# The Newton step of the reciprocal root in three VectorE instructions instead of four

## The chip, the cores and the metric

The kernel runs on one core of a Trainium2 chip. A core has a matrix engine (PE, whose weight loads are shown apart as PEld), a vector engine (DVE), an activation engine (ACT) and a general engine (POOL), all with instruction queues of their own that are worked off in order; SP's queue issues nearly all transfers (DMA). Intermediate values lie in SBUF (128 partitions) and in PSUM, where PE writes. The metric is the device time of one execution in microseconds (us); lower is better. The time stated is the median of several executions.

## The reference

The input `x` has 4 sequences of 256 tokens with 256 features, so 1024 tokens. Two decoder layers add to it, each with attention, a state-space block (mamba) that reads a second input `ctx_1024`, and a feed-forward part, each after a layer norm. All is float32. The change touches two places where a reciprocal square root is needed. The first is layer 0's attention, whose heads of 32 features are normalised (8 query, 2 key and 2 value heads):

```python
def _layernorm_unit(x, eps=EPS):
    mu = jnp.mean(x, axis=-1, keepdims=True)
    xc = x - mu
    var = jnp.mean(xc * xc, axis=-1, keepdims=True)
    return xc * jax.lax.rsqrt(var + eps)
...
q = _layernorm_unit(q) * SCALAR
k = _layernorm_unit(k)
v = _layernorm_unit(v)
```

The second is layer 1's mixture of 32 experts, of which 6 act on each token:

```python
def step(acc, ew):
    w1, w2, g = ew
    h = jnp.square(jax.nn.relu(xf @ w1.T)) @ w2.T
    return (acc + g[:, None] * h, None)
```

The kernel multiplies the hidden units by the square root of the gate `g` before they are squared, so it needs `sqrt(g)`, which it makes as `g * rsqrt(g)`.

## The kernel before, in words

Tokens lie in 8 tiles of 128 on the partitions; a batch (one sequence) is two tiles. The source calls the instructions in an order that serves as their priority. A scheduler then sets the order of each engine's queue when the kernel is built, by its own estimates of durations and by when operands and buffers come free; at run time each queue is fixed. So a change in some instructions can move others on every queue.

*Layer 0, first stage* (about 25 to 190 us of the profile). For each of the 4 batches `head0(b)` normalises the batch (`ln_transposed`), makes queries, keys and values on PE (L393), rotates them on DVE (L403, L409, L410), takes the mean away (L417, L418), sums the squares (L425, L426) and calls `rsqrt_steps` on the 24 variances of each token pair (2 tiles x 12 heads: a tile of 128x24). The results scale the queries (L433, `qn`) and values (L436, `vn`) on DVE and the keys (L440, `krep`, two instructions per batch) on POOL. `tail0(b)` transposes qn and krep on PE (L461, L466), copies them out on ACT (L471, `qkT`), and makes the scores (L486, L490), tanh (L499) and exp (L507) on ACT, the weighted sums (L513, L523, L524) on PE, the division on DVE (L449 `rden`, L450 `at`), the output projection (L543) and the addition to `x` (L551).

Into this are woven the scans of layer 0's mamba block, 16 states x 2 halves x 2 pairs of batches. A state is: decay on ACT (L238), input product `db` on POOL (L240), the scan on DVE (L241), its product `hc` on DVE (L243); the states are summed by turns on PE (L258) and on POOL (L260 here, L250 in layer 1). Their rows `bt` and `ct` are spread by DMA (L232). `mamba_front` prepares a pair of batches (convolution L189, L202, L203, dt L211 and L213, `du` L216).

*Layer 0's feed-forward* runs in two halves of two batches. For each batch the gate `sz` (ACT, L275) is multiplied on (L286), transposed back and added (L288, L294); then the norm follows: statistics on DVE (L121, L122), four small POOL instructions (L125 to L128), the normalised batch on ACT (L137), transposes on PE (L141), a copy on ACT (L144). Then come the matmuls L643 and L669. The weights of this part take the place of the attention's, so SP's loads L618 (`downs`), L620 (`gw`), L622 (`uw`) and L624 (`dw`) wait for the last projection L543; `dw` is multiplied by `downs` on POOL (L625).

*Layer 1* has attention with 16 heads of 128 features (L714 projections, L734 to L748 rotation, L812 to L845 scores and softmax, L868/L869 weighted sums, L883 output), its scans woven in, and then the experts in two halves (`moe(0)` and `moe(1)`, 512 tokens each). `moe` computes gates (`route`), clamps them (L985), calls `rsqrt_steps` on a tile of 128x128 (4 tiles of tokens x 32 experts), multiplies by the gate (L987), transposes the result on PE (L990), copies it (L992) and writes it to DRAM (L993), from where a row per expert is spread over the partitions (L1006, `gr`). The experts' matmuls are L1015 and L1029, with L1020 on DVE and L1021 on ACT between them.

`rsqrt_steps(v, n)` begins with a start value from the bits of `v` (L105) and makes three Newton steps of four DVE instructions each (L109 to L112) on two small tiles, `rs_r` and `rs_t`. It is called six times: four times with 24 columns, twice with 128.

Of the kernel before, what the change touches and what calls it, by code (L numbers as in the profile page):

```python
# [14 lines left out]
ALU = mybir.AluOpType  # L15
# [26 lines left out]
def decoder_kernel(  # L42
# [27 lines left out]
    nc = tc.nc  # L70
# [30 lines left out]
    def rsqrt_steps(v, n):  # L101

        r_ = small.tile([P, n], F32, tag=f"rs_r{n}", name="rs_r")
        t_ = small.tile([P, n], F32, tag=f"rs_t{n}", name="rs_t")
        nc.vector.tensor_scalar(  # L105
            r_.bitcast(I32), v.bitcast(I32), -0.5, float(0x5F3759DF), ALU.mult, ALU.add
        )
        for _ in range(3):
            nc.vector.tensor_mul(t_, r_, r_)  # L109
            nc.vector.tensor_mul(t_, t_, v)  # L110
            nc.vector.tensor_scalar(t_, t_, -0.5, 1.5, ALU.mult, ALU.add)
            nc.vector.tensor_mul(r_, r_, t_)  # L112
        return r_


# [234 lines left out]
    with ExitStack() as ph:  # L350
# [33 lines left out]
        def head0(b):  # L384
# [40 lines left out]
            nc.vector.tensor_reduce(rs24, sq, AX.X, ALU.add)  # L425
            nc.vector.tensor_scalar(rs24, rs24, 1.0 / 32, 1e-6, ALU.mult, ALU.add)  # L426
            rs = rsqrt_steps(rs24, 24).rearrange("p (c h) -> p c h", c=2)
            qn = ap.tile([P, 2, 8, 32], F32, tag="qn", name="qn")
            krep = ap.tile([P, 2, 2, 4, 32], F32, tag="krep", name="krep")
# [255 lines left out]
    with ExitStack() as ph:  # L685
# [289 lines left out]
        def moe(hf, ps_p, ps_h, acc):  # L975
# [8 lines left out]
            gpos = gp.tile([P, 4 * NE], F32, tag="gpos", name="gpos")  # L984
            nc.vector.tensor_scalar(gpos, gate.rearrange("p t e -> p (t e)"), 1e-30, None, ALU.max)  # L985
            root = rsqrt_steps(gpos, 4 * NE)
            done = nc.vector.tensor_mul(root, root, gate.rearrange("p t e -> p (t e)")).ins  # L987
            pg = ps(ps_p)
# [239 lines left out]
```

## Time and profile before

| what | value |
|---|---|
| median of 3 runs (lowest, highest) | 896.88 us (895.14, 897.36) |
| the profiled execution's own time | 899.26 us |
| its span, first to last instruction | 897.5 us |
| instructions on DVE | 1112 |
| narrow steps, 128x24: L109, L110, L111, L112, 12 each | 399, 304, 477, 284 ns mean |
| wide steps, 128x128: L109, L110, L111, L112, 6 each | 292, 292, 225, 291 ns mean |
| mean granted TensorE clock | 0.941 of full speed |

The profile is one execution. Its page gives the busy time of each engine, the span in 40 equal slices with a digit for the busy tenths of each, the chain of work that ended last, and the costliest groups of instructions. A group's line reads: source line, engine, operation, output <- inputs with partitions x elements and type, count, then busy us and mean ns of one, then idle time of that engine just before these instructions and the work that ended most of it. A line of the timeline reads: start us, duration us, engine, source line, operation, names and shapes, and in brackets the idle time before it with its releaser. "x2" means that two instructions of the same kind that followed each other are shown as one.

Narrow steps appear with durations from 0.16 us to over 1 us, which is why their means differ between lines that do the same amount of work. The profiled execution took 2.38 us more than the median; 1.76 us of its time lie outside the span.

### The profile page before, as it was taken

Reading aid. Unit: us, or ns where it says so; the run is one execution under the profiler, and the core shown is the slowest. Engines: PE = TensorE matmul, PEld = TensorE weight load, DVE = VectorE, ACT = ScalarE, POOL = GpSimd, SP = SyncE. Lnnn points to the kernel's source line nnn. Section 1 sums busy time; section 2 is a strip of 40 time slices with the busy share of each in tenths; the row PEclk is TensorE's granted clock in tenths of the full one; section 3 lists DMA queues with packets and bytes.
Section 4 is the critical chain, followed back from the end, with each engine's and each line's share of the span. In section 5 each row is a group of like instructions: output and inputs, shape, how many; then the busy total and the mean of one; then the engine's idle time right before and its main releaser. Section 6 shows DMA issues by size and latency. Waiting matters only on the chain.

```text
span 897.5 us, 10261 instructions
## 1 busy us (share of the span) xinstructions
PE 803.8 (90%) x3062; PEld 496.9 (55%) x3062; DVE 588.2 (66%) x1112; ACT 480.7 (54%) x1188; POOL 423.2 (47%) x427
## 2 busy tenths in 40 slices
PE   5788989978978989889898978997999999999997
PEld 2345656623433435546565745675666656666665
DVE  4897999775877668777759785788067676212121
ACT  5565545478848736746856693776333433211111
POOL 5654879865779624735635472422257751000000
PEclk9896889778986999999999999998999999999999
DMA  5545465672623400100110010000048743555542
GB/s 165 174 144 212 148 181 195 196 257 76 206 93 102 147 15 24 39 10 30 41 47 24 24 47 1 24 3 21 29 153 225 233 151 101 150 148 159 158 145 82
DMA packets 61015, 98.36 MB, mean 110 GB/s; under 512 B 6352, under 2 KB 26720, under 8 KB 60704
## 3 DMA queue, kind: packets, MB, share of 16 engines
q1 hardware_dynamic: 60080, 96.48, 34.4%
q10 hardware_dynamic: 880, 1.23, 0.4%
q8 instruction: 24, 0.39, 0.2%
q14 instruction: 31, 0.25, 0.1%
HBM read 96.24 MB, written 1.44 MB: 109 GB/s over the span
## 4 chain that ended last, share of the span: by engine, by line
PE 46%; DVE 12%; ACT 5%; POOL 3%; issue 3%; POOLq 0%; DVEq 0%; ACTq 0%
PE ps L1015 13%; PE ps L1029 12%; PE ps L883 5%; PE ps L714 4%; PE ps L868 2%; PE ps L821 2%; DVE ps L741 2%; DVE qs L734 1%; ACT sc L840 1%; DVE qr L742 1%; PE ps L748 1%; DVE h L241 1%; PE ps L669 1%; PE ps L643 1%; POOL sc L845 1%
## 5 line engine op out<-in xcount | busy, mean ns | idle before, releaser
L240 POOL TENSOR_TENSOR db<-bt,du 128x512 f32<-128x512 f32 x128 | 162.7, 1282 | 82.2 <-DVE h L241 57.0
L241 DVE TENSOR_TENSOR_SCAN h<-h,db 128x512 f32<-128x512 f32 x128 | 152.7, 1215 | 29.2 <-ACT h L238 28.1
L1015 PE MATMUL ps<-moe_xnT,w 128*128 128x512 f32 x272 | 128.9, 597 | 0.0
L1029 PE MATMUL ps<-w,hT 128*128 128x256 f32 x544 | 128.5, 379 | 0.0
L1020 DVE SCALAR_TENSOR_TENSOR hT<-ps,gr 128x512 f32<-128x512 f32 x64 | 44.1, 689 | 126.8 <-PE ps L1015 126.8
L238 ACT ACTIVATE h<-dt,negA 128x512 f32<-128x512 f32 x128 | 86.2, 689 | 73.5 <-DVE hc L243 71.2
L1029 PEld LDWEIGHTS ps<-w,hT 128*128 128x128 f32 x544 | 103.0, 190 | 40.2 <-issue 29.4
L1021 ACT ACTIVATE hT<-hT 128x512 f32<-128x512 f32 x68 | 42.8, 629 | 133.8 <-DVE hT L1020 133.6
L714 PE MATMUL ps<-wqkv,xnT 128*128 128x512 f32 x192 | 93.4, 598 | 8.0 <-DVE rq L706 5.6
L243 DVE TENSOR_TENSOR hc<-h,ct 128x512 f32<-128x512 f32 x128 | 84.8, 678 | 3.0 <-DMA ct<-bc 1.8
L250 POOL TENSOR_TENSOR y<-y,hc 128x512 f32<-128x512 f32 x64 | 80.8, 1272 | 8.3 <-DVE hc L243 6.4
L845 POOL TENSOR_TENSOR sc<-sc,rsum 128x512 f32<-128x512 f32 (+1 forms) x32 | 46.2, 1466 | 66.4 <-DVE rsum L843 66.3
L1015 PEld LDWEIGHTS ps<-moe_xnT,w 128*128 128x128 f32 x272 | 51.9, 192 | 36.5 <-issue 33.2
L707 POOL TENSOR_TENSOR rq<-rq,nhalf 128x8 f32<-128x8 f32 x20 | 33.0, 1651 | 80.9 <-DVE rq L706 80.7
L729 ACT ACTIVATE sq<-ps 128x128 f32<-128x128 f32 x160 | 42.4, 282 | 49.4 <-PE ps L714 49.4
L840 ACT ACTIVATE sc<-sc,nm 128x256 f32<-128x256 f32 (+1 forms) x128 | 56.7, 448 | 7.6 <-DVE nm L835 4.2
L883 PE MATMUL ps<-wo,oT 128*128 128x256 f32 x256 | 57.0, 381 | 0.0
L883 PEld LDWEIGHTS ps<-wo,oT 128*128 128x128 f32 x256 | 48.1, 190 | 8.9 <-ACT oT L876 2.6
L714 PEld LDWEIGHTS ps<-wqkv,xnT 128*128 128x128 f32 x192 | 32.7, 190 | 30.1 <-issue 17.5
L258 PE MATMUL ps<-hc,ident 128*128 128x512 f32 x64 | 39.9, 712 | 8.8 <-DVE hc L243 8.8
L260 POOL TENSOR_TENSOR y<-y,hc 128x512 f32<-128x512 f32 x32 | 40.8, 1274 | 4.8 <-DVE rs_t L110 2.1
L748 PE MATMUL ps<-ident,qr 128*128 128x128 f32 x160 | 28.1, 293 | 13.7 <-DVE qr L742 11.8
(206 smaller groups left out, 1450.6 us busy)
## 6 DMA issues: line engine op xcount, KB each, us to landing
bt<-bc SPq DMA_DIRECT2D x96, 256.0 KB, 3.5
ct<-bc SPq DMA_DIRECT2D x96, 256.0 KB, 3.8
w<-in_w_dram SPq DMA_DIRECT2D x64, 256.0 KB, 3.7
gr<-gt SPq DMA_DIRECT2D x64, 256.0 KB, 3.4
wqkv<-in_wqkv_dram SPq DMA_DIRECT2D x1, 3072.0 KB, 11.8
wo<-in_wo_dram SPq DMA_DIRECT2D x1, 2048.0 KB, 9.3
x<-in_x_dram SPq DMA_DIRECT2D x4, 256.0 KB, 5.1
w<-in_ws_dram SPq DMA_DIRECT2D x4, 256.0 KB, 3.9
```

What stands on the lines that cost most here:

```text
L238: nc.scalar.activation(h, dt[:, c, :], AF.Exp, scale=negA[:, a : a + 1])
L240: nc.gpsimd.tensor_mul(db, bt, du[:, c, :])
L241: nc.vector.tensor_tensor_scan(h, h, db, 0.0, ALU.mult, ALU.add)
L243: nc.vector.tensor_mul(hc, h, ct)
L250: nc.gpsimd.tensor_add(y[:, c, :], y[:, c, :], state(n, c, bt, ct))
L714: mm(pq, lhsT=xnT[:, f, c * P : (c + 1) * P], rhs=wqkv1[:, f, ch * 512 : (ch + 1) * 512], start=(f == 0), stop=(f == 1),)
L840: nc.scalar.activation(part, part, AF.Exp, bias=nm[:, qc, j : j + 1], accum_out=rsum[:, qc, j : j + 1])
L845: nc.gpsimd.tensor_mul(part, part, rsum[:, qc, :].unsqueeze(2).to_broadcast([P, 4, w]))
L883: mm(pout[:, c * 256 : (c + 1) * 256], lhsT=oTs[h // 4][:, h % 4, c * P : (c + 1) * P], rhs=wo1[:, 8 * gp + h, :], start=(h == 0), stop=(h ...
L1015: mm(ph_, lhsT=w[:, f * P : (f + 1) * P], rhs=xnT[:, f, :], start=(f == 0), stop=(f == 1))
L1020: gated.append(nc.vector.scalar_tensor_tensor(h, ph_, 0.0, g, ALU.max, ALU.mult).ins)
L1029: mm(po[t // 2][:, (t % 2) * 256 : (t % 2 + 1) * 256], lhsT=h[:, t * P : (t + 1) * P], rhs=w[:, 256:512], start=start and t % 2 == 0, stop ...
```

## The change

Each Newton step is `r <- r * (1.5 - 0.5 * v * r * r)`. Before, DVE squares `r`, multiplies by `v`, forms `-0.5 t + 1.5` and multiplies by `r`. After, the factor -0.5 is taken into the square and the addition of 1.5 into the last product, each with the instruction that applies a scalar and then a second tensor (`scalar_tensor_tensor`):

```diff
         for _ in range(3):
-            nc.vector.tensor_mul(t_, r_, r_)
+            nc.vector.scalar_tensor_tensor(t_, r_, -0.5, r_, ALU.mult, ALU.mult)
             nc.vector.tensor_mul(t_, t_, v)
-            nc.vector.tensor_scalar(t_, t_, -0.5, 1.5, ALU.mult, ALU.add)
-            nc.vector.tensor_mul(r_, r_, t_)
+            nc.vector.scalar_tensor_tensor(r_, t_, 1.5, r_, ALU.add, ALU.mult)
         return r_
```

The start value L105, the three rounds, the tiles and the callers stay. Six calls with three rounds each make 18 instructions less: twelve of 128x24 in layer 0's first stage and six of 128x128 in `moe`.

## Prediction

> **What bounds the kernel now.** I read the page first: the busy times, the 40 slices (22.4 us each) and the chain that ended last.
>
> ```profile
> PE 803.8 (90%) x3062; PEld 496.9 (55%) x3062; DVE 588.2 (66%) x1112; ACT 480.7 (54%) x1188; POOL 423.2 (47%) x427
> ...
> PE   5788989978978989889898978997999999999997
> ...
> DVE  4897999775877668777759785788067676212121
> ...
> PE 46%; DVE 12%; ACT 5%; POOL 3%; issue 3%; POOLq 0%; DVEq 0%; ACTq 0%
> ```
>
> PE is the engine of the whole; the last third is its expert matmuls without a gap. DVE, which the change relieves, counts only where its digits are 9: slices 3 to 8, the first stage, where the four `head0` calls lie. Busy times per stretch (the windows view: us of 30 for PE, PEld, DVE, ACT and POOL, then the granted clock) show that stage more finely:
>
> ```profile
> 90.00:120.00 30.00, 27.05 (x148) 19.87 (x147) 29.82 (x46) 16.50 (x39) 21.77 (x18) 0.84 0.50 159
> 120.00:150.00 30.00, 27.00 (x156) 17.46 (x156) 28.46 (x44) 14.86 (x39) 28.88 (x25) 0.90 0.58 183
> ```
>
> DVE is full in the first; in the second POOL is as full (28.88 of 30). Time taken from DVE before 120 us can become time, but must still get past POOL. Then the groups with different shapes kept apart (busy us, mean ns):
>
> ```profile
> L111 DVE TENSOR_SCALAR rs_t<-rs_t 128x24 f32<-128x24 f32 x12 | 5.7, 477 | 0.1
> ...
> L109 DVE TENSOR_TENSOR rs_t<-rs_r 128x24 f32<-128x24 f32 x12 | 4.8, 399 | 0.1
> ...
> L110 DVE TENSOR_TENSOR rs_t<-rs_t,a_rs 128x24 f32<-128x24 f32 x12 | 3.6, 304 | 0.1
> ...
> L111 DVE TENSOR_SCALAR rs_t<-rs_t 128x128 f32<-128x128 f32 x6 | 1.4, 225 | 0.2
> ...
> L961 DVE SCALAR_TENSOR_TENSOR gate<-em,room 128x128 f32<-128x128 f32 x2 | 0.6, 292 | 0.1
> ```
>
> The means of the narrow steps mislead. The timeline of DVE, and POOL's beside it, show why (start, duration):
>
> ```profile
> 43.58 0.17 DVE L110 TENSOR_TENSOR rs_t<-rs_t,a_rs 128x24 f32<-128x24 f32 x1
> 43.67 0.49 DVE L409 TENSOR_TENSOR ps<-ps,cst 128x320 f32<-128x320 f32 x1
> 44.07 1.03 DVE L111 TENSOR_SCALAR rs_t<-rs_t 128x24 f32<-128x24 f32 x1
> 45.02 1.21 DVE L335 TENSOR_TENSOR diag<-ident,par 128x1024 f32<-128x1024 f32 x1
> ```
> ```profile
> 43.80 1.27 POOL L260 TENSOR_TENSOR y<-y,hc 128x512 f32<-128x512 f32 x1 [1.28 <-DVE rs_t L110]
> ```
>
> A step costs 0.17 us; the L111 at 44.07 took 1.03 because it ended with POOL's L260 (43.80 + 1.27 = 45.07). Removing a step that stood in such a hold hands the hold to the next instruction that has all its operands in SBUF.
>
> **The change part by part.** Twelve 128x24 steps go (4 calls of `head0`, 3 Newton steps each) and six 128x128 (2 calls of `moe`).
>
> *Price of the new form.* The trace has no step with a scalar between two narrow tensors. From below: a 128x24 L110 unheld, 0.17 us; from above: L961, the same form at 128x128, 0.292. L961 costs exactly what the tensor_tensor steps of its size cost (L109, L110 at 128x128: 292 and 292 ns), so I take no extra.
>
> The Trainium skill says otherwise ("Vector Engine (DVE) Microarchitecture Reference", "Points that are easy to get wrong"): this form halves its throughput when both tensors are SBUF and not bf16. By that rule, with 1.22 ns per column from the rows ((292 - 165) / 104), the twelve wide new steps cost 0.156 us more each and the twenty-four narrow ones 0.03: about 0.9 us on `moe` 0's path and 0.7 us in the first stage, and the sum below would read 896.0. L961 speaks against the rule, and I go by L961.
>
> *First stage, the steps themselves.* From start to the next start the twelve narrow L111 take 0.17, 0.95, 0.44, 0.91, 0.08, 0.95, 0.21, 0.21, 0.09, 0.07, 0.62 and 0.24 us: 4.94 in all. Seven are unheld (1.07 us, gone for good); five are held (3.87), and of those only some 0.09 each is the step's own. Surely gone: 1.07 + 5 x 0.09 = 1.5 us.
>
> *First stage, the order.* The scheduler sets each queue's order when the kernel is built, so the shorter chains move other work. In the changed kernel as built, batch 0's qn and vn (L433, L436) stand one scan earlier on DVE, ahead of L417, L418 and a L243; POOL's two krep (L440) and PE's transposes (L461, L466) of that batch move up likewise. This aims at two idle times of before. PE waited 3.23 us (72.38 to 75.61) for L450, which stood behind L433, L436 and a L418 that took 1.36 us beside krep; and DVE, with nothing left to do, waited for PE:
>
> ```profile
> 83.56 0.17 DVE L112 TENSOR_TENSOR rs_r<-rs_r,rs_t 128x24 f32<-128x24 f32 x1
> 87.85 0.21 DVE L449 RECIPROCAL rden<-ps 128x8 f32<-128x8 f32 x1 [4.12 <-PE ps L524]
> ```
>
> I let the 4.12 us go: L449's matmuls come some 4 us earlier if batch 0's tail does. The lead at the stage's end is then 1.5 + 4.1 = 5.6 us. Bounds: 1.5 (only the unheld steps) and 4.94 + 4.12 = 9.1. What is late next there is POOL's L240/L260 stream.
>
> *Start of the first FFN half, the give-back.* Where attention releases its pool (last L543, ends 184.58 + 1.03 = 185.61), SP issues downs, gw, uw and dw. POOL scales dw (L625), and here the order turns against the change: before, the norm of batch 0 (L125 to L128) came first; after, as built, L625 stands ahead of it.
>
> ```profile
> 194.86 0.22 POOL L125 TENSOR_SCALAR ln_nb<-ln_mv 128x2 f32<-128x2 f32 x1 [3.32 <-DVE ln_mv L122]
> ...
> 197.89 3.59 POOL L625 TENSOR_TENSOR dw<-dw,downs 128x1536 f32<-128x1536 f32 x1 [0.24 <-DMA dw<-in_down_dram]
> ```
>
> So POOL blocks on dw's landing, and the norm, L137 on ACT and the transposes L141 behind it queue up. dw is ready 197.89 - 185.61 = 12.28 us after the last L543; then 3.59 for L625, 1.60 for the norm (194.86 to L137's 196.46), 0.65 from L137 to L141 (208.12 to 208.77, the second time). L141 would start at 185.61 + 12.28 + 3.59 + 1.60 + 0.65 = 203.73, against 200.67 before, where it stood behind L211: +3.1 us. From L141 to the first FFN matmul it is 11.0 us, unchanged, with the same order on every engine. All of it moves with the last L543, so the lead comes off: 3.1 - 5.6 = -2.5 us at the FFN's start. ACT also gets two more table loads there (1.28 us each, two others go away near 75 us): they delay L203 and the dt matmuls, at most to 200.67 + 2.56 - 5.6 = 197.6, earlier than L141's 203.73 - 5.6 = 198.1; hidden by the dw wait, and 2.56 us on the path if that wait is gone.
>
> *From there to the end* the orders are equal up to the roots in `moe`, and the stretch is tied through PE; I carry the -2.5 through.
>
> *`moe` 0.* The chain of waits runs through its root (604.07 to 607.46). Before, the last L112 and L987 had been put behind sixteen attention instructions; after, they stand in the chain, ahead of L814. From the first L109 to L814: 607.61 - 604.33 = 3.28 us before; after, nine steps and L987 at 0.325 each (start to start in this chain): 3.25. No gain. The transposes L990 wait in PE's order until 621.77 either way. Price 0; if PE came sooner it would be at most 0.8 (three L111 at 0.26).
>
> *`moe` 1.* 758 to 763 us, under an unbroken row of matmuls (749 to 897): 0, and if that cover were gone, 0.8.
>
> **Sum.** -2.5 us. The profiled execution took 899.26 us (span 897.5), 2.4 above the median; it would take 896.8, and the median 896.88 becomes 894.4. What a measurement here tells from no change is 0.3%, 2.7 us.
>
> **The rivals.**
>
> *A, the sum:* 894.4; by the bounds of the lead (9.1 and 1.5) 890.9 to 898.5.
>
> *B, slower: POOL swallows the lead and dw keeps its price.* Place: 120 to 190 us, where POOL is 96% busy for 30 us and the trace has DVE's holds ending with POOL's instructions. If POOL sets the pace, the last L543 stays, the lead is 0, and the norm still waits for dw: +3.1, 900.0. It is slower by the bound once the lead is under 0.4 us. For it: the window row, and two krep (0.94 us each) now ahead of scan products. Against: POOL was busy only 21.77 of 30 in the window before, so it has room to start early.
>
> *C, the dw wait does not bite:* its load lands earlier, with less traffic in front, or the scheduler's place for it hurts nobody. The lead stays whole, less what the table loads then cost at most: 5.6 to 3.0 off, 891.3 to 893.9; I take 891.3.
>
> *D, nothing arrives:* lead and give-back cancel, or PE, busy 24 to 27 of every 30 us at a clock of 0.75 to 0.90, sets the stage anyway and the norm has slack: 897.
>
> **How the numbers follow.** A 0.40, B 0.29, C 0.17, D 0.14. A straddles the bound of 0.3% (faster is under 894.2): 0.22 faster, 0.15 same, 0.03 slower, as orders that a build moves also lose. C is faster, D the same but for 0.01, B slower. Together faster 0.40, same 0.28, slower 0.32. The 8 in 10: from 890.5, just under the largest lead, to 901.5, B with half of the table loads (1.3 us) on top. A's own range is 890.9 to 898.5.
>
> **What the profile after would show.** DVE with 1094 instructions. The new narrow steps at 0.17 us unheld, the wide ones at 0.29 (0.45 would prove the skill's rule). The 3.23 us of PE at 72 us and DVE's 4.12 at 84 us gone or shrunk; the last L543 near 180 instead of 185.6. L625 before the norm of batch 0, with POOL idle until dw lands; L137 12.28 + 3.59 + 1.6 us after the last L543; first FFN matmul near 209. L987 right behind the last step of the root, L990 still far later. I am wrong if the last L543 does not come earlier (B), if L137 does not wait behind L625 (C), or if the distance from the first FFN matmul to the end changes by more than 1 us, which none of my steps provides for.

## The result and the profile after

The changed kernel takes 903.09 us (median of 5 runs, 900.37 to 904.33) against 896.88 us before (5 runs, 891.43 to 897.36): a ratio of 1.0071, 95% interval 1.0044 to 1.0098. It is slower by 6.2 us. The forecast was 894.4 us, and the range ended at 901.5.

The page of the profile after (an execution of 900.98 us, span 899.2): busy times, then the slices of PE and DVE, then the chain that ended last.

```profile
PE 793.7 (88%) x3062; PEld 491.6 (55%) x3062; DVE 589.0 (66%) x1094; ACT 480.5 (53%) x1188; POOL 421.5 (47%) x427
...
PE   5689789958977989789898978997899999999997
...
DVE  4997899875878668768759785787157776212121
...
PE 46%; DVE 12%; ACT 5%; POOL 3%; issue 3%; DVEq 0%; ACTq 0%; POOLq 0%
```

DVE has lost 18 instructions (1112 to 1094), but not busy time: 588.2 us before, 589.0 after. The groups with shapes kept apart say why (busy us, mean ns; in the changed kernel L109 and L111 are the new form, L110 the product with `v`, and later lines stand one lower than before):

```profile
L109 DVE SCALAR_TENSOR_TENSOR rs_t<-rs_r 128x24 f32<-128x24 f32 x12 | 5.5, 461 | 0.0
L435 DVE TENSOR_TENSOR vn<-r,rs_r 128x128 f32<-128x128 f32 x4 | 4.3, 1086 | 0.0
L110 DVE TENSOR_TENSOR rs_t<-rs_t,a_rs 128x24 f32<-128x24 f32 x12 | 4.1, 344 | 0.0
...
L607 DVE TENSOR_SCALAR wmean<-wmean 128x10 f32<-128x10 f32 x4 | 3.7, 928 | 0.0
L111 DVE SCALAR_TENSOR_TENSOR rs_r<-rs_t,rs_r 128x24 f32<-128x24 f32 x12 | 2.7, 222 | 0.0
L110 DVE TENSOR_TENSOR rs_t<-rs_t,gpos 128x128 f32<-128x128 f32 x6 | 1.8, 292 | 0.2
L111 DVE SCALAR_TENSOR_TENSOR rs_r<-rs_t,rs_r 128x128 f32<-128x128 f32 x6 | 1.8, 292 | 0.2
L109 DVE SCALAR_TENSOR_TENSOR rs_t<-rs_r 128x128 f32<-128x128 f32 x6 | 1.7, 290 | 0.2
```

The wide new form costs 290 to 292 ns, like the plain product. But the values `vn` went from 697 to 1086 ns each, and the small `wmean` scaling from 420 to 928; before they read:

```profile
L436 DVE TENSOR_TENSOR vn<-r,rs_r 128x128 f32<-128x128 f32 x4 | 2.8, 697 | 0.0
L608 DVE TENSOR_SCALAR wmean<-wmean 128x10 f32<-128x10 f32 x4 | 1.7, 420 | 0.0
```

The holds beside POOL have moved to other instructions. To measure them I took, for each DVE instruction of the first stage (24 us to the last L551), what it took beyond the fastest of its own form, where that was over 0.08 us: 13.5 us in all before, 14.4 after.

The milestones of both profiles, in us from the start: where the additions L551 and the first FFN matmul L643 start, where the last L543 ends, the distance from there to L643, and where the last addition to `x`, L1051, starts (lines as before the change):

| | L551 of batches 0, 1, 2, 3 | last L543 ends | first L643 | distance | last L1051 |
|---|---|---|---|---|---|
| before | 95.3, 132.5, 157.5, 185.6 | 185.6 | 211.7 | 26.1 | 892.9 |
| after | 88.2, 133.8, 160.9, 182.7 | 182.7 | 213.7 | 31.0 | 894.6 |

Batch 0 is done 7 us earlier, as hoped. By batch 1 the lead is gone, and behind the last L543 another 5 us are lost. From L643 to the last L1051 it is 681.2 us before and 680.9 after, so in these two profiles everything happens before 214 us. (In the profiles below with the same order from there on, this part took 679 to 684 us; it varies a little from one execution to the next.) The two profiled executions differ by only 1.7 us where the medians differ by 6.2; how that comes is told with the first experiment.

Where the lead goes, DVE's timeline of the changed kernel shows:

```profile
91.04 1.17 DVE L607 TENSOR_SCALAR wmean<-wmean 128x10 f32<-128x10 f32 x1
92.11 1.47 DVE L606 TENSOR_REDUCE wmean<-wqkv 128x10 f32<-128x1280 f32 x1
93.51 2.33 DVE L240 TENSOR_TENSOR_SCAN h<-h,db 128x512 f32<-128x512 f32 x2
95.75 1.26 DVE L242 TENSOR_TENSOR hc<-h,ct 128x512 f32<-128x512 f32 x2
...
103.94 0.49 DVE L402 TENSOR_TENSOR rr<-ps,cst 128x320 f32<-128x320 f32 x1 [3.41 <-PE ps L392]
```

And PE's:

```profile
96.47 1.51 PE L257 MATMUL ps<-hc,ident 128*128 128x512 f32 x2 [2.17 <-DVE hc L242]
...
101.00 2.91 PE L392 MATMUL ps<-wqkv,xnT 128*128 128x384 f32 x4
```

The same four matmuls in the kernel before:

```profile
96.11 1.45 PE L393 MATMUL ps<-wqkv,xnT 128*128 128x384 f32 x4
```

In the changed kernel PE waits 2.17 us for `hc`, which stands behind weight means and scans; a little later its granted clock is 0.50 (98 to 104 us; 1.00 before), the four L392 take 2.91 us where they took 1.45 before, and now DVE waits 3.41 us for PE. The idle times of before (PE 3.23 us at 72 us, DVE 4.12 at 84) did go or shrink (the latter to 2.97 us at 80); these came in their place.

Behind the last L543, POOL first, then DVE, ACT and PE of the changed kernel:

```profile
193.05 3.42 POOL L624 TENSOR_TENSOR dw<-dw,downs 128x1536 f32<-128x1536 f32 x1 [1.66 <-PE ps L210]
196.93 0.22 POOL L124 TENSOR_SCALAR ln_nb<-ln_mv 128x2 f32<-128x2 f32 x1 [0.46 <-DVE ln_mv L121]
```
```profile
193.71 3.04 DVE L285 TENSOR_TENSOR yg<-y,sz 128x256 f32<-128x256 f32 x1
196.67 0.17 DVE L121 BATCH_NORM_AGGREGATE ln_mv<-ln_st 128x2 f32<-128x6 f32 x1
196.76 1.19 DVE L240 TENSOR_TENSOR_SCAN h<-h,db 128x512 f32<-128x512 f32 x1
```
```profile
198.53 1.09 ACT L136 ACTIVATE xn<-x,ln_nb,ln_rs 128x256 f32<-128x256 f32 x2 [4.09 <-POOL ln_nb L127]
```
```profile
198.73 2.07 PE L257 MATMUL ps<-hc,ident 128*128 128x512 f32 x2 [5.72 <-DVE hc L242]
200.74 2.07 PE L210 MATMUL ps<-xdbl,dtproj 8*128 8x512 f32 x2
202.74 1.11 PE L140 MATMUL ps<-ident,xn 128*128 128x128 f32 x4
```

The same `yg` in the kernel before:

```profile
194.28 0.39 DVE L286 TENSOR_TENSOR yg<-y,sz 128x256 f32<-128x256 f32 x1
```

While POOL scales `dw`, DVE's `yg` is held for 3.04 us (0.39 before). Behind it wait the statistics, the scan, `hc`, PE's L257 and, in PE's order, the transposes L140 that lead to the FFN. POOL was idle 1.66 us before L624. The line names PE as the releaser, but SP issued `dw` at 184.31 and it landed 8.6 us later, at 192.9, so POOL did wait for the load. That wait is short; what holds DVE is the scaling.

### The profile page after: what moved, and what is told of

Its sections match the earlier page's. It is cut to its first block, busy times and chain, and to the rows that moved or that the text cites. A ratio compares the mean times of both kernels' runs of the same rounds, so it can differ in the third digit from the quotient of the medians.

```text
span 899.2 us, 10229 instructions
## 1 busy us (share of the span) xinstructions
PE 793.7 (88%) x3062; PEld 491.6 (55%) x3062; DVE 589.0 (66%) x1094; ACT 480.5 (53%) x1188; POOL 421.5 (47%) x427
## 4 chain that ended last, share of the span: by engine, by line
PE 46%; DVE 12%; ACT 5%; POOL 3%; issue 3%; DVEq 0%; ACTq 0%; POOLq 0%
PE ps L1014 12%; PE ps L1028 12%; PE ps L882 5%; PE ps L713 4%; PE ps L867 2%; PE ps L820 2%; DVE ps L740 2%; ACT sc L839 1%; DVE qs L733 1%; DVE qr L741 1%; PE ps L747 1%; DVE h L240 1%; PE ps L668 1%; PE ps L642 1%; POOL sc L844 1%
## 5 line engine op out<-in xcount | busy, mean ns | idle before, releaser
L257 PE MATMUL ps<-hc,ident 128*128 128x512 f32 x64 | 38.8, 693 | 15.3 <-DVE hc L242 15.2
L747 PE MATMUL ps<-ident,qr 128*128 128x128 f32 x160 | 28.1, 294 | 14.6 <-DVE qr L741 12.7
```

## The experiments

The chain of reasons under test: the shorter step saves time; the new order of the first stage and of `dw` costs more. The rivals: the new form itself, or the wide roots in `moe`.

Comparisons are with the kernel before, whose median over the runs beside each group was 897.1, 897.0 and 896.2 us.

**The narrow calls alone.**

```diff
         for _ in range(3):
+            if n == 24:
+                nc.vector.scalar_tensor_tensor(t_, r_, -0.5, r_, ALU.mult, ALU.mult)
+                nc.vector.tensor_mul(t_, t_, v)
+                nc.vector.scalar_tensor_tensor(r_, t_, 1.5, r_, ALU.add, ALU.mult)
+                continue
             nc.vector.tensor_mul(t_, r_, r_)
```

> The new step in the four narrow calls only; the roots of the gates keep four instructions. On all engines its first stage is in the order of the changed kernel. Theory (the new order of the first stage and of dw costs the time): the whole loss is here, about 903 us, ratio 1.005 to 1.009. Rival (the wide roots in moe cost it, where L987 now stands in the chain): 896 to 898, ratio 0.998 to 1.002.

904.48 us, ratio 1.0081 (1.0046 to 1.0116): the whole loss, as the theory had it. Its first stage is in the same order as the changed kernel's, but in its profile the last L543 ends at 190.0 us instead of 182.7. The windows of 24 to 180 us (busy PE, PEld, DVE, ACT, POOL, then the granted clock) of the changed kernel and of this one:

```profile
24.00:180.00 156.00, 134.53 (x636) 83.18 (x636) 139.23 (x220) 84.91 (x175) 106.38 (x101) 0.90 0.57 180
```
```profile
24.00:180.00 156.00, 139.55 (x612) 85.34 (x610) 137.01 (x216) 80.16 (x168) 103.90 (x99) 0.82 0.54 174
```

With the same order, the granted clock was 0.90 in one execution and 0.82 in the other, and the stage was 7.3 us longer in the second. Executions of one kernel spread by that much (this one 900.23 to 909.05), so single profiles tell places, and only medians and repeated distances tell sizes. The profile after above was a fortunate one.

**The wide calls alone.**

```diff
         for _ in range(3):
+            if n != 24:
+                nc.vector.scalar_tensor_tensor(t_, r_, -0.5, r_, ALU.mult, ALU.mult)
+                nc.vector.tensor_mul(t_, t_, v)
+                nc.vector.scalar_tensor_tensor(r_, t_, 1.5, r_, ALU.add, ALU.mult)
+                continue
             nc.vector.tensor_mul(t_, r_, r_)
```

> The new step in the two wide calls only; the first stage keeps four instructions and, on all engines, the order of before. Theory (order of the first stage): 896 to 898, ratio 0.998 to 1.002. Rival (moe): 901 to 904, ratio 1.005 or more.

897.42 us, ratio 1.000 (0.9973 to 1.0027). The interval allows 2.4 us either way, and the loss of 6 us is not there: that rival falls.

**The new form in a step of four.**

```diff
-            nc.vector.tensor_mul(t_, r_, r_)
+            nc.vector.scalar_tensor_tensor(t_, r_, -0.5, r_, ALU.mult, ALU.mult)
             nc.vector.tensor_mul(t_, t_, v)
-            nc.vector.tensor_scalar(t_, t_, -0.5, 1.5, ALU.mult, ALU.add)
+            nc.vector.tensor_scalar(t_, t_, 1.5, None, ALU.add)
             nc.vector.tensor_mul(r_, r_, t_)
```

> Four instructions per step as before and in the order of before, but the first is the new form (r times -0.5 times r), and the third adds 1.5 alone. Theory (order): as before, 896 to 898, ratio 0.998 to 1.002; the narrow new form at 0.17 us unheld and the wide one at 292 ns. Rival (the new form itself is dear, half throughput): wide ones at 0.45 us, ratio 1.002 to 1.004.

898.16 us, ratio 1.0005 (0.9978 to 1.0031), and in its groups with shapes apart:

```profile
L109 DVE SCALAR_TENSOR_TENSOR rs_t<-rs_r 128x24 f32<-128x24 f32 x12 | 4.8, 397 | 0.1
...
L109 DVE SCALAR_TENSOR_TENSOR rs_t<-rs_r 128x128 f32<-128x128 f32 x6 | 1.8, 292 | 0.2
```

The same places took 399 and 292 ns with the plain product. The form has no price.

**The new step in the old order.** The edges name, for each engine, the instructions of the first stage by their place in the source's order, in the sequence of the other kernel's queue; they set order alone and wait for nothing. SKIP is empty here; where the old step is held to the new order, it names the instructions that the change removes.

```diff
+    for e, (start, order) in ORDER.items():
+        traced = [
+            i
+            for i in nc.cur_bb.bb.instructions
+            if str(i.engine) == "EngineType." + e
+            and type(i).__name__ != "BassTilePoolBoundary"
+            and i.name not in SKIP
+        ]
+        for a, b in zip(order, order[1:]):
+            tc.add_manual_dep(
+                traced[b],
+                traced[a].name,
+                mybir.DependencyInfo(mybir.DependencyClass.NoSync, mybir.DependencyReason.DATA),
+                reason="order",
+            )
```

> The changed kernel (three instructions per step everywhere), but in the first stage every engine's queue is held to the order of before by order edges between neighbours. Theory (order): the loss is gone, and the removed steps that no hold covers are won, up to 1.5 us: 895 to 897.5, ratio 0.998 to 1.001. Rival (the three-instruction step itself costs time, whatever the order): 901 to 904, ratio 1.005 or more.

892.06 us, ratio 0.9958 (0.9932 to 0.9985): faster than the kernel before, and by more than expected. The step itself gains 5 us by the medians (0.42%, 3.8 us, by the ratio) when nothing else moves. The last L543 ends at 177.3 us; in three profiles of four-instruction steps in this order it was 185.6, 182.5 and 183.9. Two lines of its DVE show the mechanism (L515 is the `rden` that waited 4.12 us before; L502 is `vn`, 697 ns before and 1086 in the changed kernel):

```profile
79.93 0.21 DVE L515 RECIPROCAL rden<-ps 128x8 f32<-128x8 f32 x1 [2.37 <-PE ps L590]
```
```profile
L502 DVE TENSOR_TENSOR vn<-r,rs_r 128x128 f32<-128x128 f32 x4 | 2.4, 592 | 0.0
```

The holds fell from 13.5 to 9.9 us. The other profiles with this order on DVE agree in sign: 13.2 and 15.1 us with four instructions (the two runs above), 11.6 with three (the run with `dw` ahead of the norm, below). So the holds of removed steps were not all handed on; some 2 to 4 us went with them.

**The old step in the new order.** The same edges, with the queues of the changed kernel.

> The four-instruction step of before, with the first stage of every engine's queue held to the order of the changed kernel by order edges between neighbours (the instructions removed by the change may stand where the scheduler puts them). Theory (the order costs, the shorter step gains): 897 plus the 11 to 12 us that lie between the changed kernel and the new step in the old order (892.1): 907 to 910, ratio 1.011 to 1.014. Rival (order and step belong together, the new order costs nothing with the old step): 896 to 900, ratio under 1.004.

911.08 us, ratio 1.0157 (1.0112 to 1.0202). Now the four corners stand, in us:

| | old order | new order |
|---|---|---|
| four instructions | 897.0 | 911.1 (ratio 1.0157) |
| three instructions | 892.1 (ratio 0.9958) | 903.1 (ratio 1.0071; 904.5 and 1.0081 with the narrow calls alone) |

The shorter step gains 4 to 5 us in the old order and 7 to 8 in the new; the new order costs 10 to 12 us with the new step and 14 with the old one. The order is what made the change a loss. Of the 14 us the one profile shows some 9 (last L543 at 188.0 us against 182.5 to 185.6, distance 31.2 against 26); where the rest lies stays open.

The profiles also part the order from the chance of the granted clock. With the new step and about the same clock (0.90 and 0.87 or 0.88 between 24 and 180 us) the last L543 ends at 182.7 and 184.9 us in the new order, but at 177.3 and 180.7 in the old.

**dw behind the norm, in the changed kernel.**

```diff
-        nc.gpsimd.tensor_mul(dw, dw, downs.unsqueeze(1).to_broadcast([P, NIC, HID]))
...
                 ln_transposed(2 * hf + bb, xnT[:, :, bb * S : (bb + 1) * S], pc)
+                if hf == 0 and bb == 0:
+                    with tc.issue_after(norms[-1]):
+                        nc.gpsimd.tensor_mul(dw, dw, downs.unsqueeze(1).to_broadcast([P, NIC, HID]))
```

> The changed kernel, with the scaling of dw (L625) put behind the norm of batch 0 on POOL, as before; all other orders are those of the changed kernel. From the last L543 to the first FFN matmul it took 31.0 us in the changed kernel and 26.0 before. Theory (dw ahead of the norm costs the whole difference): 5 us off, 898 to 899.5, ratio 1.001 to 1.003, distance 26. Rival (the weights' transfer or the table loads cost it, wherever dw stands): distance 29 or more, 901 to 904.

904.09 us, ratio 1.0079 (1.0047 to 1.0112). The distance from the last L543 to the first FFN matmul fell to 28.1 us, not to 26: `dw`'s place explains 2.9 of the 5 us. The hold of `yg` is most of that: `yg` took 0.39 us here instead of 3.04, and the transposes L142 (L140 of the changed kernel) start 17.4 us after the last L543 instead of 20.05. In the time these 2.9 us do not show; with an interval of about 3 us on either side they could hide there, so the distance is the evidence, not the time.

The other 2 us lie in what the new order leaves undone at the last L543: 45 scans are done by then on DVE, in the old order 46. So one more state stands between the last L543 and the FFN, with its decay, `db`, scan, `hc` and sum `y`. ACT, then POOL, DVE and PE of this run:

```profile
186.98 1.28 ACT L239 ACT_TABLE_LOAD   x1
188.59 0.69 ACT L239 ACTIVATE h<-dt,negA 128x512 f32<-128x512 f32 x1 [0.33 <-DVE hc L244]
189.30 1.28 ACT L276 ACT_TABLE_LOAD   x1
190.59 1.58 ACT L276 ACTIVATE sz<-x,ln_nb,ln_rs 128x256 f32<-128x256 f32 x3
192.08 0.56 ACT L204 COPY xdbl<-ps 40x512 f32<-40x512 f32 x1
```
```profile
192.16 1.44 POOL L261 TENSOR_TENSOR y<-y,hc 128x512 f32<-128x512 f32 x1
```
```profile
193.63 0.69 DVE L263 TENSOR_TENSOR y<-y,ps 128x512 f32<-128x512 f32 x1 [1.16 <-POOL y L261]
194.24 0.68 DVE L295 TENSOR_TENSOR x<-x,ps 128x512 f32<-128x512 f32 x1
```
```profile
192.53 0.69 PE L289 MATMUL ps<-ident,yg 128*128 128x128 f32 x2 [1.98 <-DVE yg L287]
193.15 2.07 PE L212 MATMUL ps<-xdbl,dtproj 8*128 8x512 f32 x2
```

DVE waits 1.16 us for that state's sum on POOL, and the addition L295 starts 9.3 us after the last L543 (184.9), where it started 7.0 after it before (L294 at 192.60 against 185.6). From there to the transposes it is 8.1 us in both. The decay also splits the four `sz`, which costs two table loads more, and `xdbl` is copied 7.2 us after the last L543 instead of 4.0. But the decay itself waited for DVE's `hc`, and PE's L212, which reads `xdbl`, starts right behind L289, which waited for DVE: the table loads are covered in this trace. No run moves the extra state alone, so this is a reading of the trace.

**dw ahead of the norm, in the old order.** The edges of the old order, with L625 put ahead of L125. (On ACT, whose edges are the same, the scheduler moved the two L219 ahead of the norm too.)

> The new step in the old order of the first stage (892.1), but with L625 ahead of the norm of batch 0 on POOL. Theory: 5 us on top, 896.5 to 898, ratio 0.999 to 1.002, distance from the last L543 to the first FFN matmul 31. Rival (dw's place costs nothing by itself): 892, ratio 0.995.

895.47 us, ratio 0.9979 (0.9951 to 1.0006); distance 28.0 us. Between theory and rival: `dw`'s place costs 2 us by the distance, 1.9 by the ratios and 3.4 by the medians; the intervals of the two times overlap. The theory's 5 was too much, since it gave `dw` what belongs to the state left behind.

The path is another one here. In the old order `yg` is past when `dw` lands and is not held (0.39 us). POOL waits for the load, the norm waits for POOL, and PE for the norm (POOL, ACT, PE):

```profile
191.44 3.42 POOL L691 TENSOR_TENSOR dw<-dw,downs 128x1536 f32<-128x1536 f32 x1 [4.79 <-DMA dw<-in_down_dram]
```
```profile
196.87 1.09 ACT L203 ACTIVATE xn<-x,ln_nb,ln_rs 128x256 f32<-128x256 f32 x2 [5.25 <-POOL ln_nb L194]
```
```profile
197.52 1.18 PE L207 MATMUL ps<-ident,xn 128*128 128x128 f32 x4 [1.67 <-ACT xn L203]
```

This is the path of the prediction: `dw` ready 10.7 us after the last L543 (180.72), and 0.65 us from `xn` to the transposes.

**The weight means out of the first stage.** The edges of the old order without L607, L608 and L610, and four edges more, each from an L654 to the L607 that is to stand behind it (by their places in the source's order on DVE).

```diff
+LATE = [(274, 240), (275, 242), (276, 244), (277, 246)]
...
-        for a, b in zip(order, order[1:]):
+        for a, b in list(zip(order, order[1:])) + (LATE if e == "DVE" else []):
```

> The new step in the old order, with the eight DVE instructions for the means of layer 1's weights (L607, L608) taken out of the first stage and put behind the second to fifth L654 of the first FFN half; L610 on POOL follows them. Theory (DVE with its holds sets the first stage): 4 x (1.48 + 0.16) and some 1 us of holds leave it, the last L543 comes 4 to 7 us earlier than in the new step in the old order, and 885 to 889 if the FFN's matmuls cover the moved work. Rival (PE or POOL sets the stage, or POOL's 10 us of L610 are then paid in the FFN half): 891 or more.

894.79 us, ratio 0.9967 (0.9939 to 0.9994). The last L543 came at 172.8, 4.5 us earlier than in the new step in the old order, as expected. That does not show that DVE sets the stage, since POOL's 10 us of L610 left it together with DVE's 7.6 (5.9 of L607, 1.7 of L608). But from the first FFN matmul to the first L677 it took 43.6 us instead of 35.1. The windows of that stretch, first with the means in their old place, then with them moved there (43 us):

```profile
203.00:238.00 35.00, 34.42 (x87) 15.82 (x87) 25.25 (x31) 31.20 (x37) 24.06 (x22) 0.95 0.59 180
```
```profile
199.00:242.00 43.00, 37.17 (x87) 16.67 (x88) 35.07 (x39) 32.13 (x38) 36.47 (x31) 0.92 0.51 152
```

PE is no longer full: POOL's 10 us of L610 stand before the `db` of scans whose results PE's queue waits for. What the first stage won was paid in the next. Whether more was paid is not clear: the loss against 892.1 is 2.7 us by the medians and 0.8 by the ratios. The rival's second half was right.

**New order up to batch 0, then old; and the reverse.** The edges of both orders joined at the end of batch 0's attention.

> The new step. Every queue is held to the new order up to the end of batch 0's attention (its L551) and to the old order from there on, dw's place included. The new step in the old order reached the last L543 at 177 to 181 us and took 892.1; in the new order it was 183 to 190 and 903 to 904.5. Theory P (the new order loses before batch 0 is done: its early L551 is bought with work put off): last L543 at 183 or later, then 26 us to the first FFN matmul, 897 to 900, ratio 1.000 to 1.003. Theory Q (the loss arises after batch 0, in the new places of the weight means and the holds there): last L543 at 177 to 181, 890 to 894, ratio 0.993 to 0.997.

897.39 us, ratio 0.9984 (0.9955 to 1.0012); last L543 at 186.7, distance 26.1.

> The new step. Every queue is held to the old order up to the end of batch 0's attention, and to the new order from there on, dw ahead of the norm included. Theory P: last L543 at 177 to 181, then 31 us to the first FFN matmul: 895 to 898, ratio 0.998 to 1.001. Theory Q: last L543 at 183 or later, 902 to 905, ratio 1.005 to 1.009.

898.62 us (898.27 without its slowest execution), ratio 1.0009 (0.9982 to 1.0036); last L543 at 184.2, distance 29.2. `dw` came later in this profile than in the changed kernel (L625 starts 11.2 us after the last L543, not 10.4), and `yg` was not held (0.39 us).

Against 892.1 the first part costs 5.3 us by the medians and 2.3 by the ratios, the second 6.2 and 4.6 (3.1 of them in the distance). The interval of the first overlaps that of the new step in the old order (0.9932 to 0.9985), so its cost rests mostly on the last L543, 186.7 us against 177.3 and 180.7, in a profile with a granted clock of 0.83. Both parts seem to cost, and whether they add up to the whole cost of the order is not shown. Neither theory had it all. The first kernel's last L543 is as late as P said, though by its ratio it lost less; the second's is later than P's 177 to 181 us.

In the first, batch 0's L551 starts at 88.9 us, where it starts at 87.2 and 89.9 us in the two profiles of the old order with the new step. By then DVE has done two `hc`, one `du` and one weight mean (L607 and L608) less and one rotation instruction (L403) more, some 3.1 us of work, and POOL two L610 and one `db` less. The same counts hold between the changed kernel and the kernel before. The early end of batch 0 was no lead.

**The weight means at their old places in the new order.** The edges of the new order, with L607, L608 and L610 behind the neighbours that they have in the old one.

> The changed kernel in its new order, but the weight means (L607, L608 on DVE, L610 on POOL) stand behind the same neighbours as in the old order, so that three of the four no longer fall into 85 to 100 us. Theory Q in its first form (the crowd of weight means after batch 0 makes PE run dry): the last L543 comes back to 177 to 181, 896 to 899, ratio 0.999 to 1.002. Otherwise (the crowd is not the cause): last L543 at 183 or later, 902 to 905, ratio 1.005 to 1.009.

911.33 us, ratio 1.0138 (1.0105 to 1.017); last L543 at 197.4. The crowd of weight means after batch 0 is not the cause: putting the means back made things worse by 7 to 8 us, although the holds were few (11.8 us). Its profile, of the slowest of six executions (915.48 us), shows the other lever, a PE at a granted clock of 0.76; DVE waited 20.7 us for PE in this window, in the changed kernel 8.5:

```profile
24.00:180.00 156.00, 139.53 (x575) 84.50 (x574) 127.11 (x202) 75.55 (x159) 95.83 (x90) 0.76 0.50 164
```

Which single move in the first stage costs the time stays open; no one place that I tried carries it. DVE's time can be counted, though. From 24 us to the last L543, with the new step, DVE was idle for 18.4, 20.8 and 24.9 us in the three profiles of the new order and for 14.7 and 16.9 in the two of the old, and held for 14.4, 14.3 and 13.9 us against 9.9 and 11.6. By the means that is 5.6 us more idle time and 3.4 more of holds, less 1.9 for the scan and `hc` that the new order leaves for later: 7.1 us, where the last L543 ends 6.9 us later. The waits that grew are those for PE: 8.5, 10.4 and 15.8 us in the new order, 3.5 and 4.9 in the old. PE in turn waits for DVE, and its granted clock differs too; whether its waits lower the clock, these runs do not show.

## Why the prediction was wrong, step by step

*The price of the new form:* right. 290 to 292 ns wide, as L961 said; a step of four with it takes the same time as before. The halved throughput that the Trainium skill states for this form ("Vector Engine (DVE) Microarchitecture Reference", "Points that are easy to get wrong") would have been 0.45 us by my estimate; no run shows it.

*The steps themselves and the 4.12 us of idle time, together 5.6 us:* about the right size for the shorter step, but only where the order stays. There it gained 5 us (892.1 against 897.0; 3.8 by the ratio). That the sums agree is partly luck, as the split was off: I counted 3.4 us of holds as handed on, and the holds fell by 3.6 between these two profiles, while the idle time shrank by 1.75 us (4.12 to 2.37) instead of going.

*First stage, the order:* this step failed. I read the early places of batch 0's qn, vn and transposes as what frees the two idle times, and booked the lead as if it lasted to the last L543. There it was forecast at 5.6 us; it was 2.9 in the first pair of profiles, and -1.9 by the means of three profiles each (184.0 us before, with the two runs of four-instruction narrow steps in its order; 185.9 in the new order: 182.7, 184.9 and 190.0). With the 5.0 us behind the last L543 that makes some 6.9 us, and 6.2 were measured. The old order has the early end of batch 0 without the moves (87.2 and 89.9 us with the new step), and the new order costs 10 to 14 us in all, of which some 7 lie before the last L543 by the profiles (177.3 and 180.7 us in the old order with the new step, against those 185.9). The sum had no term for the work of the other streams that the moves put off.

*The give-back at the FFN's start:* right in sign, too small: 3.1 us forecast, 5.0 measured (26.1 to 31.0). `dw`'s part was 2.0 to 2.9 us. In the changed kernel the mechanism was another: POOL did wait for `dw`'s landing, but that came 10.4 us after the last L543 instead of 12.28, and what cost time was L624's run, which holds DVE. (With `dw` ahead of the norm in the old order, the path was the one forecast.) In the sum it is the 0.65 us from L137 to L141 that failed; it was 4.2 us, because L141 stood behind L211 and the held chain. The other 2 us are again work put off: one state of the scans that the new order leaves behind the last L543. The two table loads, taken as hidden, were hidden.

*`moe` and the way to the end:* right as far as can be seen. The wide calls alone changed nothing that stands out of an interval of 2.4 us either way, and L643 to the end is the same to 0.3 us.

*The rivals:* B had the sign and the lead of nearly 0 (900.0 against 903.1), but not the reason. POOL was busy 27.02 of 30 us between 120 and 150, less than before (28.88); it did not saturate. It acted through the holds that its instructions put on DVE, and these are a part of the loss only.

## What to carry to other kernels

Where a scheduler sets the queues, a small edit is two changes, and the second, the order, can be the larger: price it apart by holding the new instructions to the old order (and the old ones to the new) before the edit itself is judged. An early milestone is a lead only if as much other work is done by then; count the instructions of the other streams up to it. Here batch 0 ended 7 us earlier with some 3 us of DVE's work put off, and the last L543 came with one state of the scans undone. The shorter step with the old order is the version to keep: 892.1 us, 0.4% under the kernel before by the ratio and 1.2% under the changed one by the medians.

## What the runs showed of the hardware

One POOL instruction of 3.42 us (L624, 128x1536) held a DVE product with all operands in SBUF (`yg`) for 3.04 us, where that form took 0.39 us otherwise. Where the same instruction met the product `du` (128x512), that took 3.84 and 3.77 us (`dw` behind the norm in the changed kernel, and ahead of it in the old order), and 0.69 otherwise.

PE's granted clock in the first stage differs from one execution of the same order to the next: 0.90, 0.87 and 0.82 between 24 and 180 us in three profiles of the new order, with the last L543 at 182.7, 184.9 and 190.0. The times of these executions, 900.98, 903.31 and 909.03 us, spread by about as much as their last L543. So one profile of each kernel (900.98 against 899.26) could show a quarter of the difference of the medians; that the clock is the cause of the spread is not shown.
